# Where layer 3's transposed input comes from: TensorE transposes, or blocks read back from DRAM and turned by VectorE one pipeline stage later

## The chip, the cores and the metric

The kernel runs as one program on one core of a Trainium2 chip. The metric is the device time of one launch in microseconds; lower is better. A profiled execution adds a trace, from which the rows below come.

## What is computed

64 graphs of 256 nodes with 256 features pass through four residual layers, each followed by a layer norm. Layer 0 is a recurrence over the 256 nodes; layers 1 to 3 work on each graph by itself. Only layers 1 to 3 matter here:

```python
x = _layernorm(x + L0(x, adj, ...))                 # recurrence over nodes
x = _layernorm(x + relu(norm_adj @ (x @ W.T + b)))  # layer 1
x = _layernorm(x + L2(x, adj, ...))                 # layer 2: one head, masked softmax
# layer 3: 8 heads, masked softmax
q = split_heads(x @ Wq + bq)
k = split_heads(x @ Wk + bk)
v = split_heads(x @ Wv + bv)
scores = jnp.einsum('bhqd,bhkd->bhqk', q, k) / np.float32(np.sqrt(HD))
scores = jnp.where(adj[:, None, :, :] > 0, scores, jnp.float32(NEG))
out = jnp.einsum('bhqk,bhkd->bhqd', jax.nn.softmax(scores, axis=-1), v)
x = _layernorm(x + out.reshape(...) @ Wo + bo)
```

Layer 3's three projections need the layer's input with features on the partitions, that is, transposed: `x` arrives as 256 nodes by 256 features.

## The kernel before, in words

The program has two parts. `_recurrence` does layer 0 for all graphs and writes its result to a DRAM tile `Hd`; it ends at about 1424 us of the trace. `_layers` then does layers 1 to 3, in fp32, and is the part that changes. (A third function, `_layer_3`, is a safe version of layer 3 that reads the DRAM tile `Yd`; it runs only where a flag says so, and did not run here.)

`_layers` is a software pipeline written out by hand. One `Graph` object holds a graph's tiles, and each of its methods issues one step. A string `ROUND` lists the steps of one round in order, as `stage.step`, and a loop over `t` issues a round after another; the scheduler is switched off (`manual_schedule`), so each engine's queue runs in exactly this order. In round `t` the stage letter says which graph a step belongs to: `N` is graph t+2, `L` t+1, `A` t, `B` t-1, `C` t-2, `E` t-3. So six graphs are in flight:

- `load_a` and `load_b` (N) bring a graph's data in. `load_blocks` (lines 1095 to 1105) loads a 256x256 matrix as 8 DMAs of 32 KB, in such a way that each 32x32 block lands at the place of its mirror image; one VectorE instruction that transposes every 32x32 block then gives the whole transpose. This is how layer 1's input (`hz`, `xz`, turned in `turn_0`, line 1112) and the adjacency (`az`, turned in `adT_v`, line 1143) are transposed today.
- L: residual and norm of layer 0, degrees, adjacency; A: layer 1 (`t_a`, `t_b`, `g`); B: layer 2 (`xT.2`, `qk2`, `v2`, `s2`, `exp2`, `w2`, `pT2`, `f2`).
- C: layer 3's first half. `norm_b.2` writes layer 3's input `y`; `keep_3` (line 1252) stores it to `Yd`; `xT.3` (`flipped`, line 1038, four TensorE transposes of 128x128 into a PSUM bank, and the ScalarE copy at line 1164) transposes it; `qk3` (line 1240) and `v3` project, `s3` (lines 1274, 1283, 1284, 1286) makes scores, mask and exponentials for four heads at a time.
- E: layer 3's second half: `o3`, `d3`, `f3`, norm, `store`.

All DMAs of this part are issued from SyncE's queue (SP), in program order: in a round the store of E, `load_a`, `keep_3`, `load_b`. Each product (`product`, line 1048: eight matmul records of one 256x256x256 product) takes one of four PSUM banks (`bank`), in turn.

Of the kernel before, what the change touches and what calls it, by code (L numbers as in the profile page):

```python
# [9 lines left out]
F32 = mybir.dt.float32  # L10
# [9 lines left out]
P = 128  # L20
# [934 lines left out]
def _layers(tc, ident, Hd, Yd, x, adj, weights, out):  # L955
# [8 lines left out]
    nc = tc.nc  # L964
    nat, W2, W3, b1_r, b2_r, b3_r, cols = weights
    B, N, D = x.shape
# [5 lines left out]
    with ExitStack() as ctx:  # L972
# [9 lines left out]
        io = ctx.enter_context(tc.tile_pool(name="l_io", bufs=3))  # L982
# [71 lines left out]
        def new(tag, t, bufs=2, shape=(P, 2, D)):  # L1054
            return work.tile(list(shape), F32, tag=tag, name=f"{tag}_{t}", bufs=bufs)
# [17 lines left out]
        class Graph:  # L1073
# [7 lines left out]
            def load_a(self):  # L1081
                b = self.b
                self.xin = io.tile([P, 2, D], F32, tag="xin", name=f"xin_{b}")
                nc.sync.dma_start(self.xin, x[b].rearrange("(c p) d -> p c d", p=P))
                self.ad = io.tile([P, 2, N], F32, tag="ad", name=f"ad_{b}", bufs=4)
                nc.sync.dma_start(self.ad, adj[b].rearrange("(c p) m -> p c m", p=P))
                self.y = io.tile([P, 2, D], F32, tag="y", name=f"y_{b}", bufs=7)
                nc.sync.dma_start(self.y, Hd[:, b, :].rearrange("(c p) d -> p c d", p=P))
                self.az = self.load_blocks("az", adj[b])

# [1 line left out]
                self.hz = self.load_blocks("hz", Hd[:, self.b, :])  # L1092
                self.xz = self.load_blocks("xz", x[self.b])

            def load_blocks(self, tag, of):

                to = io.tile([P, 2, 8, 32], F32, tag=tag, name=f"{tag}_{self.b}", bufs=3)
                for j in range(4):
                    for a in range(2):
                        at = a * P + j * 32  # L1100
                        nc.sync.dma_start(
                            to[j * 32:(j + 1) * 32, a],
                            of[:, at:at + 32].rearrange("(i r) c -> r i c", r=32),
                        )
                return to


            def residual_0(self):
                nc.gpsimd.tensor_add(self.y, self.y, self.xin)
                nc.gpsimd.tensor_add(self.hz, self.hz, self.xz)  # L1110

            def turn_0(self):
                self.xT0 = new("xT0", self.b)
                nc.vector.transpose(
                    self.xT0.rearrange("p a m -> p (a m)"),
                    self.hz.rearrange("p a i c -> p (a i c)"),
                )

            def norm_a(self, l):
                self.mv = norm_a(self.y, f"{l}_{self.b}")  # L1120
# [21 lines left out]

            def adT_v(self):

                self.turned = new("adTr", self.b)
                nc.vector.transpose(
                    self.turned.rearrange("p a m -> p (a m)"),
                    self.az.rearrange("p a i c -> p (a i c)"),
                )
                self.neg3 = new("neg3", self.b, 4)  # L1150
                nc.vector.tensor_scalar(self.neg3, self.turned, 0.0, -NEG, ALU.is_le, ALU.mult)

            def adT_s(self):
# [96 lines left out]
                setattr(self, f"qk3{s}", m)  # L1250

            def keep_3(self):
                nc.sync.dma_start(Yd[self.b], self.y)

            def bias_3(self):
                nc.gpsimd.tensor_add(self.y, self.y, rows(b3_r))
# [82 lines left out]
        ROUND = """  # L1339
            B.xT.2 E.o3 E.d3.0 B.qk2.0 C.norm_b.2 E.d3.1  # L1340
            A.t_a A.t_b B.qk2.1 B.v2 L.residual_0 B.masks L.degrees_a
            L.adT_v E.f3 L.degrees_b C.xT.3 C.keep_3 N.load_b
            L.adT_s A.g C.bias_3 L.norm_a.0
            C.qk3.0 C.qk3.1 E.norm_a.3 A.norm_a.1 L.norm_b.0 B.s2 B.exp2
            C.s3.0 C.v3 B.w2
            B.pT2 A.norm_b.1 L.turn_0 C.s3.1 E.norm_b.3 E.store B.f2
            B.norm_a.2
        """.split()
        graphs = [Graph(b) for b in range(B)]
        graphs[0].load_a()  # L1350
        graphs[0].load_b()
        for t in range(-1, B + 3):
            if 0 <= t + 2 < B:
                graphs[t + 2].load_a()
            for step in ROUND:
                who, name, *args = step.split(".")
                b = t - "NLABCE".index(who) + 2
                if 0 <= b < B:
                    getattr(graphs[b], name)(*map(int, args))

# [33 lines left out]
def _layer_3(tc, ident, Yd, adj, l3, out):  # L1394

    nc = tc.nc
    B, N, D = out.shape
    HEADS = 8
    HD = D // HEADS
    with ExitStack() as ctx:  # L1400
# [32 lines left out]
        def rows(b):  # L1433
            return b.unsqueeze(1).to_broadcast([P, 2, D])

        with tc.For_i(0, B, 1) as b:
            y = work.tile([P, 2, D], F32, name="gy")
            nc.sync.dma_start(y, Yd[b])
            ad = work.tile([P, 2, N], F32, name="gad")
            nc.sync.dma_start(ad, adj[b].rearrange("(c p) m -> p c m", p=P))  # L1440
            neg = work.tile([P, 2, N], F32, name="gneg")
            nc.vector.tensor_scalar(neg, ad, 0.0, -NEG, ALU.is_le, ALU.mult)
            xT = flip(y, "gxT")
            qk = []
            for s, n in enumerate("qk"):
                pm = product(W[n], xT, f"g{n}_ps")
                m = work.tile([P, 2, N], F32, name=f"g{n}")
                for c in range(2):
                    nc.vector.tensor_scalar(m[:, c, :], pm[:, c, :], cols[:, s, c:c + 1], None, ALU.add)
                qk.append(m)  # L1450
            v = work.tile([P, 2, D], F32, name="gv")
            nc.vector.tensor_add(v, product(xT, W["v"], "gv_ps"), rows(row["v"]))
            o = work.tile([P, 2, D], F32, name="go")
            for h in range(HEADS):
                hc, i = divmod(h, P // HD)
                r = slice(i * HD, (i + 1) * HD)
                pm = ps.tile([P, 2, N], F32, tag="mm", name=f"gs_ps_{h}")
                for c in range(2):
                    nc.tensor.matmul(
                        pm[:, c, :], qk[0][r, hc, c * P:(c + 1) * P], qk[1][r, hc, :],  # L1460
                        start=True, stop=True,
                    )
                sm = work.tile([P, 2, N], F32, tag="gs", name=f"gs_{h}")
                nc.vector.tensor_add(sm, pm, neg)
                mx = work.tile([P, 2], F32, tag="gmx", name=f"gmx_{h}")
                nc.vector.tensor_reduce(mx, sm, AX.X, ALU.max)
                sums = work.tile([P, 2], F32, tag="gsums", name=f"gsums_{h}")
                for c in range(2):
                    nc.vector.tensor_scalar(
                        sm[:, c, :], sm[:, c, :], mx[:, c:c + 1], None, ALU.subtract  # L1470
                    )
                nc.scalar.activation(sm, sm, AF.Exp, scale=1.0 / math.sqrt(HD))
                nc.vector.tensor_reduce(sums, sm, AX.X, ALU.add)
                nc.vector.reciprocal(sums, sums)
                pT = flip(sm, "gpT")
                po = ps.tile([P, 2, HD], F32, tag="po", name=f"go_ps_{h}")
                for c in range(2):
                    for k in range(2):
                        nc.tensor.matmul(
                            po[:, c, :], pT[:, k, c * P:(c + 1) * P],  # L1480
                            v[:, k, h * HD:(h + 1) * HD], start=(k == 0), stop=(k == 1),
                        )
                    nc.vector.tensor_scalar(
                        o[:, c, h * HD:(h + 1) * HD], po[:, c, :], sums[:, c:c + 1], None, ALU.mult
                    )
            pm = product(flip(o, "goT"), W["o"], "gf_ps")
            nc.gpsimd.tensor_add(y, y, rows(row["o"]))
            nc.vector.tensor_add(y, y, pm)
            for c in range(2):
                st = work.tile([P, 6], F32, tag="gst", name=f"gst_{c}")  # L1490
                mv = work.tile([P, 2], F32, tag="gmv", name=f"gmv_{c}")
                rstd = work.tile([P, 1], F32, tag="grstd", name=f"grstd_{c}")
                nc.vector.bn_stats(st, y[:, c, :])
                nc.vector.bn_aggr(mv, st)
                nc.vector.tensor_scalar(rstd, mv[:, 1:2], EPS, None, ALU.add)
                nc.gpsimd.tensor_tensor(rstd, rstd, mhalf[:, 0:1], ALU.pow)
                nc.vector.tensor_scalar(
                    y[:, c, :], y[:, c, :], mv[:, 0:1], rstd, ALU.subtract, ALU.mult
                )
            nc.sync.dma_start(out[b].rearrange("(c p) d -> p c d", p=P), y)  # L1500
# [3 lines left out]
def kernel(ctx: ExitStack, tc: tile.TileContext, ins, out):  # L1504
    nc = tc.nc
    x, adj = ins["x"], ins["adj"]
    B, N, D = x.shape
    main = ctx.enter_context(tc.tile_pool(name="main", bufs=1))
    dram = ctx.enter_context(tc.tile_pool(name="dram", bufs=1, space=bass.MemoryType.DRAM))
# [18 lines left out]
        )),  # L1528
        wide, load_layers,
    )  # L1530
    Yd = dram.tile([B, P, 2, D], F32, name="Yd")
    found = _layers(tc, ident, Hd, Yd, x, adj, weights, out)
    with tc.If(found > 0):
        _layer_3(tc, ident, Yd, adj, l3, out)
# [36 lines left out]
```

## Time and profile before

| | us |
|---|---|
| median of 3 runs | 3260.26 (3257.63 to 3262.72) |
| the profiled execution, its own time | 3263.34 |
| its span, first to last instruction | 3261.6 |
| end of the recurrence's last matmuls in the trace | 1423 |
| one round of the layers, full pipeline | 27.50 |
| busy share of the span: PE, DVE, ACT, POOL | 94%, 79%, 61%, 58% |
| busy share of 2400 to 2600 us: PE, DVE, ACT, POOL | 100%, 89%, 66%, 53% |

PE is TensorE (PEld its weight loads), DVE VectorE, ACT ScalarE, POOL GpSimd, SPq SyncE's DMA queue. The spans of the whole program mix two parts with different limits, so a change in the layers is read in rows from that part: from about 1440 us on, in rounds.

### The profile page before, as it was taken

Reading aid. Unit: us, or ns where it says so; the run is one execution under the profiler, and the core shown is the slowest. Engines: PE = TensorE matmul, PEld = TensorE weight load, DVE = VectorE, ACT = ScalarE, POOL = GpSimd, SP = SyncE. Lnnn points to the kernel's source line nnn. Section 1 sums busy time; section 2 is a strip of 40 time slices with the busy share of each in tenths; the row PEclk is TensorE's granted clock in tenths of the full one; section 3 lists DMA queues with packets and bytes.
Section 4 is the critical chain, followed back from the end, with each engine's and each line's share of the span. In section 5 each row is a group of like instructions: output and inputs, shape, how many; then the busy total and the mean of one; then the engine's idle time right before and its main releaser. Section 6 shows DMA issues by size and latency. Waiting matters only on the chain.

```text
span 3261.6 us, 80661 instructions
## 1 busy us (share of the span) xinstructions
PE 3057.9 (94%) x28332; PEld 2274.2 (70%) x28332; DVE 2585.9 (79%) x7361; ACT 1987.3 (61%) x5224; POOL 1884.5 (58%) x2226
## 2 busy tenths in 40 slices
PE   4799999999899998959999999999999999999997
PEld 3566666655566655637888888888888888888885
DVE  2477777877677878746888888888988888888885
ACT  0166666666566666635666666666666666666664
POOL 2276777777677878724555555555555555555543
PEclk8899999999999999979999999999999999999999
DMA  9866777787776764333333333333333333333310
GB/s 304 245 166 147 191 175 184 168 181 195 174 190 149 189 157 134 90 73 80 75 75 76 75 78 78 79 78 79 78 79 79 79 79 78 79 77 79 77 42 21
DMA packets 806735, 385.76 MB, mean 118 GB/s; under 512 B 525260, under 2 KB 774232, under 8 KB 802648
## 3 DMA queue, kind: packets, MB, share of 16 engines
q1 hardware_dynamic: 788312, 362.61, 46.3%
q10 hardware_dynamic: 18016, 17.96, 1.7%
q8 instruction: 226, 3.70, 0.5%
q14 instruction: 181, 1.48, 0.2%
HBM read 261.75 MB, written 99.61 MB: 111 GB/s over the span
## 4 chain that ended last, share of the span: by engine, by line
PE 82%; DMA 7%; DVE 6%; issue 2%; SPq 1%; ACT 1%; POOL 1%; ACTq 0%; DVEq 0%; POOLq 0%
PE mm L1048 14%; PE rc L620 7%; PE rc L612 5%; PE s L1274 4%; PE late L531 4%; PE mm_2f L1048 4%; PE mm_3v L1048 4%; PE mm_2v L1048 3%; PE mm_3f L1048 3%; PE mm_t L1048 3%; PE mm_g L1048 3%; PE mm_2s L1048 3%; PE mm_2w L1048 3%; PE o L1309 3%; PE z_ps L620 3%; PE z_ps L612 2%
## 5 line engine op out<-in xcount | busy, mean ns | idle before, releaser
L1286 POOL TENSOR_TENSOR p3s<-p 128x256 f32<-128x256 f32 x512 | 359.1, 734 | 269.2 <-ACT p L1284 269.0
L1048 PE MATMUL mm<-xT,weights 128*128 128x256 f32 x2048 | 484.0, 385 | 2.7 <-ACT xT L1164 2.7
L696 POOL TENSOR_TENSOR ACC<-ACC,far 128x640 f32<-128x640 f32 (+2 forms) x312 | 413.4, 1325 | 83.0 <-ACT far L687 44.9
L645 DVE SCALAR_TENSOR_TENSOR ACC<-keep,S,ACC 128x128 f32<-128x128 f32 x1561 | 436.8, 343 | 14.4 <-POOL ACC L913 9.6
L1048 PEld LDWEIGHTS mm<-xT,weights 128*128 128x128 f32 x2048 | 386.2, 191 | 80.3 <-ACT xT L1164 29.3
L1283 DVE TENSOR_TENSOR p<-s,neg 128x512 f32<-128x512 f32 x512 | 317.5, 682 | 85.2 <-PE s L1274 85.2
L1004 ACT ACTIVATE y<-y,shift,rstd 128x256 f32<-128x256 f32 x512 | 279.6, 596 | 158.6 <-DVE shift L1002 158.5
L1284 ACT ACTIVATE p<-p 128x512 f32<-128x512 f32 x512 | 306.9, 629 | 3.3 <-DVE p L1283 3.0
L612 PE MATMUL rc<-WxT,xqT 128*64 128x256 f32 x2048 | 268.8, 383 | 4.3 <-ACT xqT L256 2.2
L996 POOL TENSOR_TENSOR rstd<-rstd,mhalf 128x2 f32<-128x2 f32 x256 | 173.9, 698 | 134.1 <-DVE rstd L995 132.3
L840 POOL TENSOR_TENSOR ready<-ACC,dinv 128x128 f32<-128x128 f32 x255 | 102.3, 401 | 251.9 <-DVE ACC L645 246.4
L692 POOL TENSOR_TENSOR far<-hs,S 128x384 f32<-128x384 f32 (+1 forms) x310 | 222.5, 718 | 4.7
L1323 DVE RECIPROCAL rT<-o 128x256 f32<-128x256 f32 x128 | 223.7, 1748 | 0.0
L992 DVE BATCH_NORM_STATS2 st<-y 128x6 f32<-128x256 f32 x512 | 209.6, 409 | 12.6 <-POOL y L1185 9.8
L1185 POOL TENSOR_TENSOR y<-y,g 128x512 f32<-128x512 f32 x64 | 81.2, 1269 | 216.4 <-ACT g L1182 190.2
L1196 ACT ACTIVATE qk<-mm,weights 128x256 f32<-128x256 f32 x256 | 107.4, 470 | 160.4 <-PE mm L1048 158.6
L620 PE MATMUL rc<-WhT,rT 128*64 128x128 f32 x2048 | 170.2, 287 | 29.7 <-DVE rT L863 27.7
L620 PE MATMUL rc<-WhT,xpT 128*64 128x128 f32 x2048 | 168.9, 286 | 29.3 <-ACT xpT L629 27.7
L863 DVE TENSOR_TENSOR rT<-rT_ps,xpT 128x128 f32<-128x128 f32 x256 | 74.2, 290 | 153.8 <-PE rT_ps L861 150.6
L531 PE MATMUL late<-Hw,An 64*32 64x256 f32 x3840 | 172.0, 390 | 19.4 <-DMA Hw<-hs 7.8
L620 PEld LDWEIGHTS rc<-WhT,rT 128*64 128x64 f32 x2048 | 107.9, 137 | 117.1 <-DVE rT L863 110.8
L620 PEld LDWEIGHTS rc<-WhT,xpT 128*64 128x64 f32 x2048 | 107.0, 136 | 115.1 <-ACT xpT L629 106.1
(170 smaller groups left out, 7413.1 us busy)
## 6 DMA issues: line engine op xcount, KB each, us to landing
xX<-in_x_dram ACTq DMA_DIRECT2D x16, 1024.0 KB
Us<-xu SPq DMA_DIRECT2D x64, 256.0 KB
ACC<-Us SPq DMA_DIRECT2D x32, 512.0 KB
Es<-eu SPq DMA_DIRECT2D x64, 256.0 KB
early_sb<-Es SPq DMA_DIRECT2D x32, 512.0 KB
xin<-in_x_dram SPq DMA_DIRECT2D x64, 256.0 KB
ad<-in_adj_dram SPq DMA_DIRECT2D x64, 256.0 KB
y<-Hd SPq DMA_DIRECT2D x64, 256.0 KB
```

The costliest lines, as they stand in the source:

```text
L531: nc.tensor.matmul(pb[g][q * T:(q + 1) * T, e, :], An[rows, b].rearrange("p u s -> p (u s)"), Hw[rows, b, :], start=True, stop=True,)
L612: nc.tensor.matmul(G[o * B:(o + 1) * B], xqT[a, i // 2][:, i % 2, kc, h * B:(h + 1) * B], WxT[:, kc, o, gates], start=False, stop=False, s ...
L620: nc.tensor.matmul(G[o * B:(o + 1) * B], hT[:, kc * B:(kc + 1) * B], WhT[:, kc, o, g], start=False, stop=(kc == 1), skip_group_check=True,)
L645: nc.vector.scalar_tensor_tensor(acc[:, 0, :], keep[:, j % 2, :], s, acc[:, 0, :], ALU.mult, ALU.add)
L692: nc.gpsimd.tensor_mul(tmp[:, begun:count, :], hs.unsqueeze(1).to_broadcast(shape), s[:, begun:count].unsqueeze(2).to_broadcast(shape),)
L696: nc.gpsimd.tensor_add(acc, acc, tmp[:, 0:count, :])
L1004: nc.scalar.activation(y[:, c, :], y[:, c, :], AF.Identity, bias=shift[:, c:c + 1], scale=rstd[:, c:c + 1],)
L1048: nc.tensor.matmul(pm[:, c, :], lhsT[:, k, c * P:(c + 1) * P], rhs[:, k, :], start=(k == 0), stop=(k == 1),)
L1283: nc.vector.tensor_add(p, s_ps[i], self.neg3)
L1284: nc.scalar.activation(p, p, AF.Exp, scale=ISQ)
L1286: nc.gpsimd.tensor_add(both, p[:, 0, :], p[:, 1, :])
L1323: nc.vector.reciprocal(rT, o_ps[:, 1, :])
```

## The change

Stage C no longer projects. After it has stored `y` to `Yd`, which now has the plain layout of nodes by features, `load_3` reads it back with `load_blocks` as 8 DMAs of 32 KB into a new tile `yz`, and `turn_3` turns its blocks with one VectorE instruction, right behind layer 1's `turn_0` and before the second group of scores. The four TensorE transposes and the ScalarE copy of `xT.3` are gone. A new stage `D` (graph t-3) takes over `qk3`, `s3` and `v3`, and `E` becomes graph t-4; the loop runs one round more, and `y` and `neg3` have one more buffer. The transposition of `hz` and `az` goes through a common helper `turn`, with the same instruction as before.

```diff
-                self.y = io.tile([P, 2, D], F32, tag="y", name=f"y_{b}", bufs=7)
+                self.y = io.tile([P, 2, D], F32, tag="y", name=f"y_{b}", bufs=8)
...
+            def turn(self, tag, blocks):
+                t = new(tag, self.b)
+                nc.vector.transpose(
+                    t.rearrange("p a m -> p (a m)"), blocks.rearrange("p a i c -> p (a i c)")
+                )
+                return t
...
-                self.neg3 = new("neg3", self.b, 4)
+                self.neg3 = new("neg3", self.b, 5)
...
             def keep_3(self):
-                nc.sync.dma_start(Yd[self.b], self.y)
+                nc.sync.dma_start(Yd[self.b].rearrange("(c p) d -> p c d", p=P), self.y)
+
+            def load_3(self):
+                self.yz = self.load_blocks("yz", Yd[self.b], 2)
+
+            def turn_3(self):
+                self.xT_sb = self.turn("xT3", self.yz)
...
         ROUND = """
             B.xT.2 E.o3 E.d3.0 B.qk2.0 C.norm_b.2 E.d3.1
             A.t_a A.t_b B.qk2.1 B.v2 L.residual_0 B.masks L.degrees_a
-            L.adT_v E.f3 L.degrees_b C.xT.3 C.keep_3 N.load_b
-            L.adT_s A.g C.bias_3 L.norm_a.0
-            C.qk3.0 C.qk3.1 E.norm_a.3 A.norm_a.1 L.norm_b.0 B.s2 B.exp2
-            C.s3.0 C.v3 B.w2
-            B.pT2 A.norm_b.1 L.turn_0 C.s3.1 E.norm_b.3 E.store B.f2
+            L.adT_v E.f3 L.degrees_b C.keep_3 N.load_b
+            L.adT_s A.g C.load_3 C.bias_3 L.norm_a.0
+            D.qk3.0 D.qk3.1 E.norm_a.3 A.norm_a.1 L.norm_b.0 B.s2 B.exp2
+            D.s3.0 D.v3 B.w2
+            B.pT2 A.norm_b.1 L.turn_0 C.turn_3 D.s3.1 E.norm_b.3 E.store B.f2
             B.norm_a.2
         """.split()
...
-        for t in range(-1, B + 3):
+        for t in range(-1, B + 4):
...
-                b = t - "NLABCE".index(who) + 2
+                b = t - "NLABCDE".index(who) + 2
...
-    Yd = dram.tile([B, P, 2, D], F32, name="Yd")
+    Yd = dram.tile([B, N, D], F32, name="Yd")
```

More of the change, by code (lines that the diff above doesn't have):

```diff
@@ L1093, in load_b, with load_blocks @@
                 self.xz = self.load_blocks("xz", x[self.b])
-            def load_blocks(self, tag, of):
-                to = io.tile([P, 2, 8, 32], F32, tag=tag, name=f"{tag}_{self.b}", bufs=3)
+            def load_blocks(self, tag, of, bufs=3):
+                to = io.tile([P, 2, 8, 32], F32, tag=tag, name=f"{tag}_{self.b}", bufs=bufs)
                 for j in range(4):
@@ L1110, in residual_0 @@
                 nc.gpsimd.tensor_add(self.hz, self.hz, self.xz)
-            def turn_0(self):
[L1113 to L1117, printed above, removed]
+            def turn(self, tag, blocks):
[4 more added lines that the diff above has]
+                return t
+            def turn_0(self):
+                self.xT0 = self.turn("xT0", self.hz)
             def norm_a(self, l):
@@ L1143, in adT_v @@
             def adT_v(self):
[L1145 to L1149, printed above, removed]
-                self.neg3 = new("neg3", self.b, 4)
+                self.turned = self.turn("adTr", self.az)
+                self.neg3 = new("neg3", self.b, 5)
                 nc.vector.tensor_scalar(self.neg3, self.turned, 0.0, -NEG, ALU.is_le, ALU.mult)
@@ L1437, in _layer_3 @@
             y = work.tile([P, 2, D], F32, name="gy")
-            nc.sync.dma_start(y, Yd[b])
+            nc.sync.dma_start(y, Yd[b].rearrange("(c p) d -> p c d", p=P))
             ad = work.tile([P, 2, N], F32, name="gad")
```

## The prediction

> **What bounds the kernel now.** First the page: the whole span, then the 40 slices, to find the part that changes.
>
> ```profile
> span 3261.6 us, 80661 instructions
> ...
> PE 3057.9 (94%) x28332; PEld 2274.2 (70%) x28332; DVE 2585.9 (79%) x7361; ACT 1987.3 (61%) x5224; POOL 1884.5 (58%) x2226
> ...
> PE   4799999999899998959999999999999999999997
> DMA  9866777787776764333333333333333333333310
> ```
>
> From slice 18 on (the layers) PE stands at 9 and DMA at 3. The busy time by stretch says how full the others are there:
>
> ```profile
> 2400.00:2600.00 200.00, 200.00 (x1354) 162.75 (x1353) 179.00 (x436) 131.72 (x282) 105.50 (x130) 1.00 0.34 80
> ```
>
> PE is never idle, DVE has 10% left, the granted clock is 1.00. A busy PE alone proves little, so next the timeline of one round on PE:
>
> ```profile
> 2324.60 1.89 PE L1048 MATMUL mm_g<-t,adT 128*128 128x256 f32 x8
> ...
> 2337.84 1.99 PE L1048 MATMUL mm_2f<-w,pT 128*128 128x256 f32 x8
> ...
> 2349.94 1.89 PE L1048 MATMUL mm_3f<-weights,oT 128*128 128x256 f32 x8
> 2351.66 0.60 PE L1038 MATMUL tr_x<-ident,y 128*128 128x128 f32 x4
> 2352.10 1.89 PE L1048 MATMUL mm_g<-t,adT 128*128 128x256 f32 x8
> ```
>
> mm_g to mm_g is 27.50 us, the round, and no PE row between carries a wait. PE is the bound, and the tr_x group between mm_3f and mm_g is what goes. How close the others follow is on DVE's and ACT's timelines:
>
> ```profile
> 2331.71 0.69 DVE L1217 TENSOR_TENSOR sm<-mm_2s,ad 128x512 f32<-128x512 f32 x1 [0.17 <-PE mm_2s L1048]
> ...
> 2336.01 0.70 DVE L1114 STREAM_TRANSPOSE xT<-hz 128x512 f32<-128x512 f32 x1
> 2337.93 2.48 DVE L1283 TENSOR_TENSOR p<-s,neg 128x512 f32<-128x512 f32 x4 [1.22 <-PE s L1274]
> ...
> 2352.03 0.71 DVE L1146 STREAM_TRANSPOSE adTr<-az 128x512 f32<-128x512 f32 x1 [0.21 <-DMA hz<-Hd]
> ```
> ```profile
> 2337.12 0.60 ACT L1230 COPY pT<-tr_p 128x512 f32<-128x512 f32 x1
> ```
>
> DVE's one real gap is 1.22 us before the second scores, right behind turn_0's transpose (2336.01): the place of turn_3. And ACT ends pT at 2337.72, only 0.12 before mm_2f needs it. Last the DMA queue, and the DMA engines a round later:
>
> ```profile
> 2348.41 0.37 SPq L1253 DMA_DIRECT2D Yd<-y  x1
> 2348.82 3.92 SPq L1101 DMA_DIRECT2D hz<-Hd  x8
> ```
> ```profile
> 2385.00:2386.00 1.00, 1.00 (x6) 0.89 (x5) 0.79 (x4) 0.83 (x2) 1.00 (x2) 1.00 0.42 67
> 2386.00:2387.00 1.00, 1.00 (x12) 0.63 (x14) 0.45 (x2) 0.43 (x1) 1.00 (x3) 1.00 0.04 6
> ```
>
> The second column from the right is the DMA share: it dies at 2386.0. Call T the start of the second scores on DVE (2337.93, then 2365.43). keep_3 is issued at T+10.48; two groups of eight block loads follow at 0.49 us each and end at T+18.75, which is 2384.18 in the next round. So the last block lands about 1.85 us after its issue.
>
> **The change part by part.**
>
> *PE: four transposes less per graph.* The groups list puts tr_x at 276 ns each, and the Trainium skill ("TensorE: Matmul & The Clock Gate", Part 4) names about 275 ns for one in a kernel. By that, four are 1.1 us and 60 full rounds 66 us. But a mean of one is not a share of the queue: mm_3f starts at 2349.94, a product takes 1.73 start to start, tr_x starts at 2351.66 and mm_g at 2352.10. Pipelined, the four cost 0.44 us. The row decides: 27.50 falls to 27.06 at best.
>
> *ACT: one copy of 0.59 less.* ACT stood idle 1.32 us just before it, so nothing is gained there. The bank that it used goes too: of 15 banks a round 14 stay, and mm_g then takes the bank that t_a's product left, which it must await anyway for t (done by 2350.64, needed at 2351.66).
>
> *DVE: one transpose of 0.70 more* (the row of turn_0, same shape). Today adT_v's transpose is held 0.21 for its eight DMA semaphores; in the order of the built kernel that wait has gone, and turn_3 carries it. DVE's own loop: 27.50 - 1.22 - 0.17 (both waits for PE) + 0.70 = 26.81. It still fits under 27.06, with 0.25 to spare. Behind turn_3 on DVE stand the second scores; for them wait ACT's exponentials, POOL's sums and PE's o3.
>
> *The mixed chain.* The same layers tie the engines crosswise: PE's second scores (end 2337.84) release DVE (0.09); DVE reaches s2 after 21.28 - 0.17 - 0.21 = 20.90; from s2 to the end of pT are 2337.72 - 2331.71 = 6.01; 0.12 to mm_2f; then one PE round of 27.06 to the scores after. Sum 54.18 for two rounds, 27.09 each. So of 0.44 about 0.41 remains. Ends: 0.44 (the 0.12 is slack) and 0.30 (adT_v's 0.21 stays). I take 0.40: 60 full rounds (t = 4 to 63) give 24.0.
>
> *SP and DMA: eight block loads more.* They stand behind load_b and before E's store. keep_3 must have landed: hz's eighth DMA today already waits for it on the same semaphore and loses nothing (3.92 for eight), so it lands in under 3.9 us. Its rows shrink from 2 KB to 1 KB; E's store has 1 KB rows and lands in time for the same wait. SP is then issuing until T+22.65; the next store is at T+4.21 of the round after (2342.14), so 8 us stay free. yz lands at T+22.65+1.85 = T+24.5. turn_3 is reached at about T+25.9 (s2 at 20.9, plus 2336.71 - 2331.71 = 5.0). Margin 1.4 us. The Trainium skill ("DMA: Bandwidth & Descriptors", Rules for kernel authors) speaks against this: small transfers are to be coalesced, since under 64 KB one pays mostly overhead, and the page's fixed cost of a DMA is about 2.0 us (fitted on GpSimd's path). Paid in series, an estimate from that page, eight cost 16 us, yz lands at T+34.8 and each round loses 9 us: slower by over 500 us. The row says that eight go out in 3.9 us and overlap, and the DMA share is 0.42 beside such loads. I take the row. It has a spread, though: in the round 1555 one group of eight took 5.26, and more than a quarter of the groups took over 4.0. Three groups lie between keep_3 and turn_3, so some rounds use up the margin. I charge 3 us for these in all (ends 0 and 10).
>
> *A stage more: fill and drain.* Rounds are counted from xT.2 to xT.2 (o3 in the drain):
>
> ```profile
> 1490.21 1.06 PE L1038 MATMUL tr_x<-ident,y 128*128 128x128 f32 x4
> ...
> 1514.46 0.60 PE L1038 MATMUL tr_x<-ident,y 128*128 128x128 f32 x4
> ```
> ```profile
> 3217.73 0.64 PE L1300 MATMUL o<-p3s,ones 128*32 128x256 f32 x8
> ...
> 3243.10 0.76 PE L1300 MATMUL o<-p3s,ones 128*32 128x256 f32 x8 [0.53 <-DVE p L1283]
> ```
>
> Round 2 takes 24.25 today. It loses layer 3's projections and scores (8 us of PE), but its softmax of layer 2 is then exposed, as in round 1 (25.52, with cold products of 3.78): estimate 23.0, so -1.3. Round 3 becomes today's round 2 without the transposes: 23.8 for 27.50, so -3.7. Round 64 loses the exposed transposes and copy, 3204.14 - 3202.87: -1.2. Round 65 took 25.37; without xT.3 (3229.48 to 3231.21) and with PE no longer cold after it (16 qk3 records took 5.89, warm 3.62): about 22.3, so -3.1. The new round has D and E of the last two graphs: o3 to mm_3f's second half as at the end of today (3243.10 to 3249.97, 6.9), its rest 1.6, qk3 3.6, then copies, scores and sums to the next o3, about 6: +18. Sum +8.7; ends +5 and +14.
>
> **Sum.** -24.0 + 8.7 + 3 = -12.3. Against the span 3261.6 that gives 3249.3 (own time 3263.34, 1.7 more). That execution lies 3.1 above the median; taken from the median, 3260.3 - 12.3 = 3248.0.
>
> **The rivals.** (1) *yz comes late.* turn_3 waits in DVE's queue, the second scores behind it, and PE stalls at o3. It decides where a block lands more than 1.85 + 1.4 + 0.25 = 3.5 us after its issue; every further microsecond costs 60. For it: the y load of 256 KB took 4.6 us in the fill, and the margin is small. Against: the DMA share falls to 0.04 at once after the blocks, and the queue would be alone then. At 4.6 us, 1.1 late: the round is 28.2, 60 x 0.7 + 8.7 = +51, 3311. At break-even (0.2 us late) 3260.
>
> (2) *The gain is eaten by the mixed chain.* DVE has 0.25 to spare, and some of its small instructions stretch beside POOL's (shift 0.16 to 0.76). If 0.3 of the 0.44 is lost to such shifts, 60 x 0.14 = 8.4 pays for the fill and drain only: 3260 to 3262. With all lost, 3269.
>
> (3) *PE takes all 0.44 and SP's spread is hidden:* -26.4 + 8.7 = -17.7, 3242.6.
>
> That the transposes stay is excluded: the built kernel's PE order has 64 groups of them fewer.
>
> **How the numbers follow.** About 0.2% (6.5 us) is what a measurement of this kernel can tell from no change. The forecast, with rival 3 at its lower end, has 0.64: 3240 to 3254. Rival 2 in the middle 0.13 (same); rival 2 entirely lost 0.09 and rival 1 0.14 (slower). Faster 0.64, same 0.13, slower 0.23. The range goes from 3240 (rival 3 with the fill and drain at their low end, less a little) to 3267 (near rival 2 lost); about 0.05 lies below, 0.15 above.
>
> **What would show it.** Right: mm_g starts 1.73 after mm_3f; the round is 27.05 to 27.2; turn_3 takes 0.70 and its wait is 0.2 to 0.3; adT_v's wait is gone; the last round is about 18 us longer in the drain. Wrong: a wait of turn_3 for yz of over half a microsecond in most rounds (rival 1); PE rows with waits for pT, for o3's sums or for xT.2's copy (rival 2); a new round of over 22 us in the drain.

## The result, and the profile after

The changed kernel takes 3242.68 us (median of 7 runs, 3236.6 to 3248.55); the kernel before, run again beside it, takes 3259.58 (3253.68 to 3268.86). The ratio is 0.9942 [0.9925, 0.9958]: faster by 0.58%, some 19 us by the ratio and 17 by the two medians. The forecast was 3248.0, a gain of 12.3. The profiled execution of the changed kernel has a span of 3239.9 us and an own time of 3241.76.

The page after (span; busy time, share of the span and instruction count by engine; the slices of PE and DMA):

```profile
span 3239.9 us, 80388 instructions
...
PE 3038.5 (94%) x28076; PEld 2257.2 (70%) x28076; DVE 2611.5 (81%) x7425; ACT 1949.4 (60%) x5160; POOL 1882.3 (58%) x2226
...
PE   4799999999999998958999999999999999999997
DMA  9866777777776764434344444444444444444421
```

PE has 256 matmul records less, four for each of 64 graphs, DVE 64 instructions more and ACT 64 less. The DMA slices of the layers rose from 3 to 4. The stretch from 2400 to 2600 us (busy time of PE, PEld, DVE, ACT and POOL, then the granted clock, the DMA share and GB/s):

```profile
2400.00:2600.00 200.00, 200.00 (x1374) 162.32 (x1366) 184.75 (x448) 129.45 (x278) 107.31 (x133) 1.00 0.41 92
```

PE is still never idle and its granted clock is still 1.00. DVE's busy time rose from 179.00 to 184.75. PE's timeline of one round after (start, busy time, operation):

```profile
2328.19 1.89 PE L1048 MATMUL mm_3f<-weights,oT 128*128 128x256 f32 x8
2329.92 1.89 PE L1048 MATMUL mm_g<-t,adT 128*128 128x256 f32 x8
...
2343.16 1.99 PE L1048 MATMUL mm_2f<-w,pT 128*128 128x256 f32 x8
...
2355.26 1.89 PE L1048 MATMUL mm_3f<-weights,oT 128*128 128x256 f32 x8
...
2356.98 1.89 PE L1048 MATMUL mm_g<-t,adT 128*128 128x256 f32 x8
```

mm_g starts 1.73 after mm_3f, where it was 2.16 with the transposes between them, and mm_g to mm_g is 27.06. DVE's timeline of that round, of the next, and up to s2 in the one after:

```profile
2329.93 0.70 DVE L1114 STREAM_TRANSPOSE adTr<-az 128x512 f32<-128x512 f32 x1
...
2337.03 0.69 DVE L1216 TENSOR_TENSOR sm<-mm_2s,ad 128x512 f32<-128x512 f32 x1
...
2341.27 0.70 DVE L1114 STREAM_TRANSPOSE xT<-hz 128x512 f32<-128x512 f32 x1
2341.90 0.66 DVE L1114 STREAM_TRANSPOSE xT<-yz 128x512 f32<-128x512 f32 x1
2343.25 2.48 DVE L1288 TENSOR_TENSOR p<-s,neg 128x512 f32<-128x512 f32 x4 [0.68 <-PE s L1279]
...
2364.09 0.69 DVE L1216 TENSOR_TENSOR sm<-mm_2s,ad 128x512 f32<-128x512 f32 x1
...
2369.80 0.71 DVE L1114 STREAM_TRANSPOSE xT<-yz 128x512 f32<-128x512 f32 x1 [0.77 <-DMA yz<-Yd]
2370.44 2.45 DVE L1288 TENSOR_TENSOR p<-s,neg 128x512 f32<-128x512 f32 x4
...
2391.16 0.69 DVE L1216 TENSOR_TENSOR sm<-mm_2s,ad 128x512 f32<-128x512 f32 x1
```

adT_v's wait of 0.21 is gone. turn_3 sits in the gap ahead of the second scores, and 0.68 us of that gap is still there. The third group of rows shows the next round, in which the block loads come late: turn_3 waits 0.77, and the scores follow at once, without a wait of their own. The lateness used up the gap and 0.13 us more (2343.25 to 2370.44 is 27.19), and DVE made that up before s2: 20.72 us from the scores to s2, where it had taken 20.84 a round earlier (2343.25 to 2364.09). PE's next round is 27.07. Over the steady part, 1600 to 3100 us, the list of waits has (us in total, times, longest):

```profile
DVE p L1288 <- PE s L1279: 30.1, 47, 0.7
...
DVE xT L1114 <- DMA yz<-Yd: 4.8, 8, 0.9
```

DVE waits for PE 47 times and for the read-back 8 times; three more waits of turn_3, 1.2 us together, stand in the list without a named releaser. PE leads.

**Where the 19 us lie in the two traces.** From the first xT.2 to the end the layers took 1796.9 us before and 1777.9 after: 19.0 less. The 60 full rounds have a mean of 27.506 before and 27.075 after, which makes 25.8; fill and drain give 6.8 back. The recurrence, which the change does not touch, ended 1.9 us earlier in this trace. Its last matmuls ended between 1411.4 and 1429.8 us in the traces of the kernels that share it, so single runs differ by several microseconds for that alone.

The fill and the drain (PE rows of the changed kernel; xT.2 of rounds 2, 3 and 4, then o3 of the last three rounds):

```profile
1487.31 1.06 PE L1038 MATMUL tr_x<-ident,y 128*128 128x128 f32 x4
...
1509.09 0.60 PE L1038 MATMUL tr_x<-ident,y 128*128 128x128 f32 x4
...
1532.45 0.60 PE L1038 MATMUL tr_x<-ident,y 128*128 128x128 f32 x4
```
```profile
3180.93 0.64 PE L1305 MATMUL o<-p3s,ones 128*32 128x256 f32 x8
...
3203.41 0.70 PE L1305 MATMUL o<-p3s,ones 128*32 128x256 f32 x8 [0.53 <-DVE p L1288]
...
3221.24 0.69 PE L1305 MATMUL o<-p3s,ones 128*32 128x256 f32 x8 [0.53 <-DVE p L1288]
```

Round 2 takes 21.78 (24.25 before), round 3 23.36 (27.50), round 65 22.48 (25.37), and the new round 17.83.

### The profile page after: what moved, and what is told of

It reads as the page before. It is cut to its first block, busy times and chain, and to the rows that moved or that the text cites. A ratio compares the mean times of both kernels' runs of the same rounds, so it can differ in the third digit from the quotient of the medians.

```text
span 3239.9 us, 80388 instructions
## 1 busy us (share of the span) xinstructions
PE 3038.5 (94%) x28076; PEld 2257.2 (70%) x28076; DVE 2611.5 (81%) x7425; ACT 1949.4 (60%) x5160; POOL 1882.3 (58%) x2226
## 4 chain that ended last, share of the span: by engine, by line
PE 83%; DVE 6%; DMA 5%; issue 2%; SPq 1%; POOL 1%; ACT 1%; ACTq 0%; DVEq 0%; POOLq 0%
PE mm L1048 14%; PE rc L620 8%; PE rc L612 5%; PE late L531 4%; PE s L1279 4%; PE mm_2f L1048 4%; PE mm_3v L1048 4%; PE mm_2v L1048 3%; PE mm_t L1048 3%; PE mm_g L1048 3%; PE mm_3f L1048 3%; PE mm_2s L1048 3%; PE mm_2w L1048 3%; PE o L1314 3%; PE z_ps L620 3%; PE z_ps L612 3%
```

## The experiments

All ratios are to the kernel before, run on the same chip, with a 95% interval.

**1. The stage alone.** Stage D and the extra round stay, but the TensorE transposes come back and nothing is read back or turned.

```diff
-            L.adT_v E.f3 L.degrees_b C.keep_3 N.load_b
-            L.adT_s A.g C.load_3 C.bias_3 L.norm_a.0
+            L.adT_v E.f3 L.degrees_b C.xT.3 C.keep_3 N.load_b
+            L.adT_s A.g C.bias_3 L.norm_a.0
...
-            B.pT2 A.norm_b.1 L.turn_0 C.turn_3 D.s3.1 E.norm_b.3 E.store B.f2
+            B.pT2 A.norm_b.1 L.turn_0 D.s3.1 E.norm_b.3 E.store B.f2
```

> Stage D and the extra round stay, but the four TensorE transposes and the ScalarE copy of layer 3's input are kept in stage C, and nothing is read back. My theory: the gain comes from the 0.44 us that the transposes take in PE's queue, the extra stage only costs. Then the full round is back at 27.50 us, and the layers are longer than before by the fill and drain alone: rounds 2 and 3 shorter by 2 to 6 us together, rounds 64 and 65 by 2 to 4, the new round 17 to 18 longer. In all +7 to +10 us against the kernel before, ratio 1.002 to 1.003. Rival: the gain comes from the stage itself, since the projections no longer wait for a transpose made just ahead of them; then the round falls below 27.3 here too and the kernel is faster than before.

Measured: 1.0040 [1.0022, 1.0058], 3274.13. PE's timeline:

```profile
2319.90 1.89 PE L1048 MATMUL mm_g<-t,adT 128*128 128x256 f32 x8
...
2345.24 1.89 PE L1048 MATMUL mm_3f<-weights,oT 128*128 128x256 f32 x8
...
2347.40 1.89 PE L1048 MATMUL mm_g<-t,adT 128*128 128x256 f32 x8
```

The round is 27.50 again and mm_3f to mm_g 2.16. So the stage by itself is a pure cost, some 12 us by its trace and 12 by its median, rather more than the sum's 8.7; all of the gain comes from the transposes that leave PE's queue. (The ScalarE copy came back with them. But the whole difference, 2.16 against 1.73, lies between the starts of mm_3f and mm_g, where mm_3f and the transposes alone stand.)

**2. The read-back left out.** turn_3 turns the blocks of `y` itself, so it waits for no DMA. Layer 3's input is then not the true transpose; its shape and cost are the same.

```diff
-            L.adT_s A.g C.load_3 C.bias_3 L.norm_a.0
+            L.adT_s A.g C.bias_3 L.norm_a.0
...
-                self.xT_sb = self.turn("xT3", self.yz)
+                self.xT_sb = new("xT3", self.b)
+                nc.vector.transpose(
+                    self.xT_sb.rearrange("p a m -> p (a m)"),
+                    self.y.rearrange("p a m -> p (a m)"),
+                )
```

> As the changed kernel, but nothing is read back: turn_3 turns the blocks of y as they stand in SBUF (so layer 3's input is not properly transposed: its values are left out of account, its shape and cost are the same). It takes away the eight block loads per graph and their wait. My theory: the read-back is hidden, so the round stays 27.06 to 27.07 and the time is that of the changed kernel within 2 us (ratio to before 0.994). The prediction charged 3 us for late blocks; if that charge is real, this kernel is 3 to 10 us faster than the changed one (ratio 0.991 to 0.993).

Measured: 0.9950 [0.9931, 0.9969], 3245.91; mean round 27.10. Taking away 512 DMAs gains nothing that these intervals, some 6 us to each side, can show. But one thing came with it: adT_v's wait for its DMA semaphores, gone in the changed kernel, is back, at 0.20 us in most rounds. So the price of the read-back alone is better read in the trace of the changed kernel: of its 60 full rounds three are over 27.1: 27.50 (round 4), 27.15 and 27.13, each behind a turn_3 that came late, by 1.27, 0.85 and 0.84 us. That is 0.6 us in all, where 3 us had been charged. (Round 4 takes 27.06 here, without the read-back.)

Some rounds of this run are longer still. DVE's row of one of them, then PE's:

```profile
2333.56 0.71 DVE L1114 STREAM_TRANSPOSE adTr<-az 128x512 f32<-128x512 f32 x1 [0.56 <-DMA hz<-Hd]
```
```profile
2346.53 1.99 PE L1048 MATMUL mm_2f<-w,pT 128*128 128x256 f32 x8 [0.28 <-ACT pT L1229]
```

This is the mixed chain of the forecast, seen at its edge: DVE is held ahead of s2, pT is late, and PE waits for it. In most rounds, with the wait of 0.20, DVE needs 20.95 us from the second scores to s2, mm_2f starts 0.05 behind pT's end, and the chain gives (0.09 + 20.95 + 6.01 + 0.05 + 27.06) / 2 = 27.08; the median round is 27.09.

**3. Turned twice.** One more block transpose in DVE's gap.

```diff
+                self.turn("xT3b", self.yz)
                 self.xT_sb = self.turn("xT3", self.yz)
```

> As the changed kernel, but turn_3 turns its blocks twice into two tiles, so VectorE has 0.63 to 0.70 us more in the same gap. It asks how far VectorE is from being the bound. In the changed kernel's trace VectorE still waits 0.68 us for the second scores. My theory: VectorE's own loop is 27.06 - 0.68 = 26.4 and becomes 27.0 to 27.1 with the second turn, so the round grows by at most 0.05 us, in all 0 to 3 us over the changed kernel. The prediction's sum had 26.81 for this loop, which would give 27.5 and +26 us over the changed kernel.

Measured: 0.9956 [0.9939, 0.9974], 3245.73. The mean round is 27.15, and most rounds are 27.06 or 27.07; the 60 full rounds take 4.4 us longer than in the changed kernel, a little over the 0 to 3 expected. DVE's timeline:

```profile
2339.97 0.66 DVE L1114 STREAM_TRANSPOSE xT3b<-yz 128x512 f32<-128x512 f32 x1
2340.57 0.66 DVE L1114 STREAM_TRANSPOSE xT<-yz 128x512 f32<-128x512 f32 x1
2341.32 2.48 DVE L1289 TENSOR_TENSOR p<-s,neg 128x512 f32<-128x512 f32 x4
```

The gap before the scores is now full, yet most rounds stay where PE puts them. VectorE was not the bound in the changed kernel: it had about one more transpose to spare, as the 0.68 said. What is lost lies in the rounds with a late read-back, for which no cover is left. The latest one of the steady part:

```profile
2720.76 0.71 DVE L1114 STREAM_TRANSPOSE xT3b<-yz 128x512 f32<-128x512 f32 x1 [1.16 <-DMA yz<-Yd]
```

The round that PE begins behind it, at 2722.62, takes 28.05. (In the fill one turn is 1.70 late, and round 4 behind it takes 28.54.)

**4. The same work, placed early in the next round.** turn_3 stands ahead of adT_v, with a third buffer for `yz`; the instructions are the same ones.

```diff
-            L.adT_v E.f3 L.degrees_b C.keep_3 N.load_b
+            D.turn_3 L.adT_v E.f3 L.degrees_b C.keep_3 N.load_b
...
-            B.pT2 A.norm_b.1 L.turn_0 C.turn_3 D.s3.1 E.norm_b.3 E.store B.f2
+            B.pT2 A.norm_b.1 L.turn_0 D.s3.1 E.norm_b.3 E.store B.f2
```

> As the changed kernel, but turn_3 is moved: it is done in the next round ahead of adT_v's transpose (yz has three buffers), so the same instruction stands in VectorE's queue before s2 instead of behind it. VectorE's total is unchanged and yz is there long before. My theory, the mixed chain: from the second scores to s2 VectorE then needs 20.84 + 0.70 + about 0.2 for the wait = 21.7, and (0.09 + 21.7 + 6.01 + 0.12 + 27.06) / 2 = 27.5 per round: the whole gain of the transposes is lost, +26 us over the changed kernel, ratio to before 1.002; PE rows show a wait for pT ahead of mm_2f in every other round. Rival: only each engine's own loop counts, PE 27.06 and VectorE under 27; then the round stays 27.06 and the time is that of the changed kernel.

Measured: 1.0002 [0.9989, 1.0014], 3264.10: the whole gain is gone, although PE and DVE do the same work. PE's timeline over three rounds:

```profile
2302.15 1.99 PE L1048 MATMUL mm_2f<-w,pT 128*128 128x256 f32 x8 [0.93 <-ACT pT L1229]
...
2329.21 1.99 PE L1048 MATMUL mm_2f<-w,pT 128*128 128x256 f32 x8
...
2356.91 1.99 PE L1048 MATMUL mm_2f<-w,pT 128*128 128x256 f32 x8 [0.57 <-ACT pT L1229]
```

27.06, then 27.70, in turn: every second round PE waits for pT. DVE's timeline ahead of the last row, and ScalarE's row of pT, show where it comes from:

```profile
2329.30 2.48 DVE L1288 TENSOR_TENSOR p<-s,neg 128x512 f32<-128x512 f32 x4 [1.28 <-PE s L1279]
...
2343.34 0.71 DVE L1114 STREAM_TRANSPOSE xT<-yz 128x512 f32<-128x512 f32 x1 [0.20 <-DMA hz<-Hd]
...
2350.85 0.69 DVE L1216 TENSOR_TENSOR sm<-mm_2s,ad 128x512 f32<-128x512 f32 x1
```
```profile
2356.26 0.60 ACT L1229 COPY pT<-tr_p 128x512 f32<-128x512 f32 x1
```

From the second scores to s2 DVE now needs 21.55 us (2329.30 to 2350.85), where 20.72 were enough in the changed kernel: turn_3 and its wait lie inside the chain instead of in the gap behind it. pT ends at 2356.86, and PE, which waits for it, starts mm_2f 0.05 later. The chain gives (0.09 + 21.55 + 6.01 + 0.05 + 27.06) / 2 = 27.38, the mean round measured. The theory's 27.5 had taken 21.7 and 0.12 for two of these. That the chain binds is shown by PE's wait for pT in every second round; the sum says how much it takes.

**5 and 6. The read-back made late.** Four, then eight, more block loads are issued ahead of those of `yz`, into a tile that nothing reads.

```diff
             def load_3(self):
+                more = io.tile([P, 2, 8, 32], F32, tag="yw", name=f"yw_{self.b}", bufs=2)
+                for j in range(2):
+                    for a in range(2):
+                        at = a * P + j * 32
+                        nc.sync.dma_start(
+                            more[j * 32:(j + 1) * 32, a],
+                            Yd[self.b][:, at:at + 32].rearrange("(i r) c -> r i c", r=32),
+                        )
                 self.yz = self.load_blocks("yz", Yd[self.b], 2)
```

(`range(4)` in the second.)

> As the changed kernel, but load_3 issues four more block loads of the same graph (32 KB each, into a tile that nothing reads) ahead of yz's eight. It makes yz later by 4 x 0.49 = 1.96 us and changes nothing else. My theory: in the changed kernel yz lands at about T+25.4 and turn_3 is reached at T+25.7, so yz is now 1.6 us late; VectorE has 0.68 us to spare before the second scores, and the rest goes on the round: 27.06 + 0.9 = 28.0, in 60 rounds about +55 us over the changed kernel, ratio to before 1.010 to 1.014, with turn_3 waiting 1.5 us in nearly every round. Rival: the block loads drain faster than they are issued and the lateness is smaller than the issue time; then under +25 us.

> The same with eight more block loads ahead of yz, 3.92 us. My theory: each microsecond of lateness past the spare costs 60 us, so another 1.96 us on the round against four more: 29.9 to 30.0, about +170 us over the changed kernel, ratio to before 1.045 to 1.050. Rival: the loop through SyncE's queue closes (the store of E waits, load_a and keep_3 come later, and yz with them), and the cost grows faster than the added issue time: over +200 us.

Measured: 1.0164 [1.0144, 1.0185], 3314.97, with four; 1.0522 [1.0504, 1.0541], 3432.63, with eight. SP's timeline with four more, and the turn behind it on DVE's:

```profile
2333.79 1.93 SPq L1259 DMA_DIRECT2D yw<-Yd  x4
2335.77 5.06 SPq L1101 DMA_DIRECT2D yz<-Yd  x8
```
```profile
2342.47 0.71 DVE L1114 STREAM_TRANSPOSE xT<-yz 128x512 f32<-128x512 f32 x1 [1.79 <-DMA yz<-Yd]
```

The last load was issued at 2340.83 and the turn ran at 2342.47, 1.64 later. The waits, first with four more loads, then with eight:

```profile
DVE xT L1114 <- DMA yz<-Yd: 98.6, 51, 3.1
```
```profile
DVE xT L1114 <- DMA yz<-Yd: 190.8, 49, 5.1
```

That is 1.93 and 3.89 us a round. Less DVE's gap of 0.68, times 60: 75 and 193 us over the changed kernel. Measured, by the ratios: 0.0222 and 0.0580 of 3260, 72 and 189. From four to eight the ratio rises by 0.0358, 117 us, for 1.96 us more of issue: 60 for each, the price that rival 1 was given. Both ratios came out above what was expected of them, since turn_3 waits longer than was thought: 1.93 us with four more, where 1.5 was expected. Rival 1's mechanism exists and its price was right; the change stops just short of the point from which it decides.

**7. A further version: layer 2's input in the same way.** xT.2's transposes leave PE too (another stage X, another eight loads, another turn, two more rounds in all than before; the block tiles have two buffers instead of three, and load_b comes last). DVE is relieved: the degrees' row sums go to ScalarE and neg3 to GpSimd.

```diff
+            def load_2(self):
+                self.yz2 = self.load_blocks("yz2", Yd[self.b], 2)
+
+            def turn_2(self):
+                self.xT_sb = self.turn("xT2", self.yz2)
...
-                nc.vector.tensor_reduce(deg, self.ad, AX.X, ALU.add)
+                junk = work.tile([P, N], F32, tag="junk", name=f"junk_{b}", bufs=1)
+                for c in range(2):
+                    nc.scalar.activation(junk, self.ad[:, c, :], AF.Copy, accum_out=deg[:, c:c + 1])
...
-            B.xT.2 E.o3 E.d3.0 B.qk2.0 C.norm_b.2 E.d3.1
+            E.o3 L.sums E.d3.0 B.qk2.0 C.norm_b.2 E.d3.1
...
-            B.pT2 A.norm_b.1 L.turn_0 C.turn_3 D.s3.1 E.norm_b.3 E.store B.f2
+            B.pT2 A.norm_b.1 A.keep_2 L.turn_0 X.turn_2 C.turn_3 D.s3.1 E.norm_b.3 E.store B.f2
```

> A version that carries the change on: layer 2's input is stored, read back and turned by VectorE in the same way (one more stage X, load_2 behind keep_3, load_b last), so xT.2's four transposes leave PE too. VectorE is relieved in return: the degrees' row sums go to ScalarE, neg3 to GpSimd. My theory: PE's round is 27.06 - 0.53 = 26.53; from the second scores to s2 VectorE needs about 20.84 - 0.71 - 0.34 = 19.8, so the mixed chain gives (0.09 + 19.8 + 6.01 + 0.12 + 26.53) / 2 = 26.3, below PE's round; VectorE's own loop is 26.4 - 1.05 + 0.65 = 26.0. 60 rounds x 0.53 = -32 us, the further stage +9 to +13: about -20 us against the changed kernel, ratio to before 0.987 to 0.990. Rival: SyncE's queue, busy 22.6 of 26.5 us a round then, or late blocks become the bound; then the round stays above 27 us and the kernel is slower than the changed one by the stage alone, about +10 us.

Measured: 0.9937 [0.9919, 0.9955], 3245.63: no better than the changed kernel, and neither the theory nor its rival expected it. The theory took 0.53 for xT.2's transposes, from their start to o3's. But mm_2f to o3 is 1.93 without them and was 2.36 with them (2343.16 to 2345.52 in the changed kernel), so 0.43 to 0.44 is what leaves the queue; and the round is 26.91, not 27.06 - 0.44 = 26.62. PE's timeline, and GpSimd's:

```profile
2333.08 0.64 PE L1319 MATMUL o<-p3s,ones 128*32 128x256 f32 x8
...
2335.26 0.89 PE L1319 MATMUL o<-p3s,ones 128*32 128x256 f32 x8
2336.08 1.13 PE L1048 MATMUL mm<-xT,weights 128*128 128x256 f32 x4
```
```profile
2332.67 2.81 POOL L1305 TENSOR_TENSOR p3s<-p 128x256 f32<-128x256 f32 x4 [1.96 <-ACT p L1303]
```

GpSimd's sums end at 2335.48, after PE reaches the second group of o3 at 2335.26; that group takes 0.89 where it took 0.61 in the changed kernel. In the changed kernel xT.2's transposes stood ahead of o3 and gave GpSimd their 0.44 us. So the instructions that left look like cover for another chain, which the next run puts to the test.

**8. The same with cover put back.** Layer 2's first projection goes ahead of o3.

```diff
-            E.o3 L.sums E.d3.0 B.qk2.0 C.norm_b.2 E.d3.1
+            B.qk2.0 E.o3 L.sums E.d3.0 C.norm_b.2 E.d3.1
```

> As the version with both inputs read back, but B.qk2.0 is issued ahead of E.o3. In that version's trace the round is 26.91 us, not 26.53: the transposes of xT.2 had covered the chain from the second scores over VectorE, ScalarE and GpSimd to o3's last sums, and without them o3's sums take 0.90 instead of 0.61 us and wait for GpSimd. A product of 1.73 us that depends on none of these now stands in that place. My theory: the wait goes and the round falls to 26.5 to 26.6, 60 x 0.35 = about -20 us against that version: ratio to before 0.987 to 0.989, about 0.6% below the changed kernel. Rival: o3 comes 1.73 us later, d3 and with it mm_3f come late, and the round stays at 26.9 or grows.

Measured: 0.9882 [0.9864, 0.9900], 3225.61: faster than both kernels. PE's timeline:

```profile
2323.24 1.99 PE L1048 MATMUL mm_2f<-w,pT 128*128 128x256 f32 x8
2325.07 1.89 PE L1048 MATMUL mm<-xT,weights 128*128 128x256 f32 x8
2326.89 0.64 PE L1319 MATMUL o<-p3s,ones 128*32 128x256 f32 x8
...
2329.07 0.61 PE L1319 MATMUL o<-p3s,ones 128*32 128x256 f32 x8
...
2349.86 1.99 PE L1048 MATMUL mm_2f<-w,pT 128*128 128x256 f32 x8
```

o3's second group is back at 0.61 and the round is 26.62, 0.44 under the changed kernel: again the queue time of four transposes. The 0.29 that run 7 lacked came back with the cover alone. Runs 7 and 8 carry several edits at once; what the moves to ScalarE and GpSimd are worth singly was not tried.

## Why the prediction was right, and where its sizes were off

The direction and the main mechanism were right: the gain is four transposes' share of PE's queue, paid for by a longer fill and drain. The time came out near the low end of the range.

- *Four transposes are 0.44 us of PE's queue, not 1.1.* Right. The 60 full rounds gave 25.8 us, 0.43 each; run 1 puts the transposes back and the 0.43 with them, and run 8 takes four others out for 0.44. At their mean duration of 276 ns the gain would have been 66 us.
- *The mixed chain leaves 0.40.* The chain exists, and runs 2 and 4 make it bind. In the changed kernel it does not bind: the usual round takes all of the 0.44, so a term of 24.0 measured 26.4 (25.8 with the late rounds, which belong to a term below). With the distances read there its sum is (0.09 + 20.84 + 6.01 + 0.12 + 27.06) / 2 = 27.06, but that proves nothing: the first four run from one mm_2f to the next, and add up to a round whatever bounds it. Two of them hold slack. From the scores to s2 20.72 is enough when DVE is late, and mm_2f can start 0.05 behind pT (run 4). Without the slack the chain is 26.97, 0.09 under PE's own 27.06. The forecast took 20.90 for the one and the full 0.12 for the other; that the 0.12 is slack was its upper end, and that is nearer the truth. (It also took 27.10 where its own working said 27.09.)
- *DVE's own loop of 26.81.* Too high by at least 0.4: the scores still wait 0.68 in a round of 27.06, so the loop is under 26.4. Part of it is that turn_3 starts 0.63 after turn_0, where the row had 0.70, and that adT_v's wait, left in the sum, is gone. turn_3 did not take that wait over: in the usual round it shows none of the 0.2 to 0.3 that were named as a sign. Run 3 confirms the spare time.
- *yz lands at T+24.5, margin 1.4.* Wrong, without consequence. The issue of `yz` ends at T+23.9 in the median round (T+22.7 to T+25.0; T is the start of the second scores on DVE), where T+22.65 was expected: the working took two groups that ended at T+18.75, close to the earliest of that trace, where the median is T+19.7. With four more loads, where the turn follows the landing in every round, the turn starts a median of 1.6 us after the last issue (1.85 was forecast), though 2.9 and 3.3 in two of 53. So yz is there at about T+25.5, and turn_3 is reached at T+25.7: a margin of 0.2. Groups of eight stretch, too: 20 of 64 groups of yz took over 4.0 us. So turn_3 waits in 11 rounds of the steady part, at most 0.9, and DVE's gap takes nearly all of that. That the read-back costs next to nothing is in part luck: two errors, the loop too long and the margin too wide, cancelled.
- *3 us for SP's spread and late blocks.* Too much: 0.6 in the trace, as told at run 2.
- *The transfers overlap and do not pay a fixed cost in series.* Right. Eight go out in 3.9 us and the last is there 1.6 us later; the serial estimate of 9 us a round does not hold here.
- *Fill and drain +8.7.* Measured +6.8 in the trace. Rounds 2 and 3 gave 6.6 where 5.0 was estimated (which of their waits went was not tested); round 64 gave 1.45 for 1.2, round 65 2.9 for 3.1 (the forecast's two parts, 1.73 and 2.27, really add up to 4.0), and the new round cost 17.83 for 18. Run 1 gives about 12 for the same stage with the transposes in, so the term depends on what else the edge rounds hold.

The three terms of the sum, chain, edges and spread, erred by 2.4, 1.9 and 2.4 us to the same side, together 6.7, the difference between the sum (-12.3) and the layers' traces (-19.0). Rival 3 (3242.6, all of the 0.44 taken and the spread hidden) is what happened, but for the 0.6 and the shorter edges. Rival 1 was near: four more loads make it the result.

## What to carry to other kernels

The mean duration of an instruction in a full queue (276 ns for a transpose here) is not what its removal gains (0.11 us each); what it gains is read from the starts of its neighbours, how far apart they are with it and without it. Where two engines tie each other over two rounds, add the chain up from rows before moving anything, and take out of each distance the wait or slack that it holds, for the distances of a full pipeline always add up to its round. Here the same 0.70 us instruction cost nothing in the gap behind the chain and the whole gain inside it. And before an instruction is taken off the bounding engine, ask which other engine it was giving time to.

## What the hardware showed that was not expected

- Of two block transposes in a row on VectorE the second starts 0.60 to 0.63 after the first and is listed with 0.66, where one alone takes 0.70.
- neg3 (a comparison with zero and a multiplication, 128x512) takes 1.93 us on GpSimd in run 7, while another tensor_scalar of the same shape (an addition and a multiplication) takes 0.62 there:

```profile
2340.49 0.62 POOL L1194 TENSOR_SCALAR neg<-ad 128x512 f32<-128x512 f32 x1
2344.99 1.93 POOL L1155 TENSOR_SCALAR neg<-adTr 128x512 f32<-128x512 f32 x1
```

- The issue of eight DMAs takes 3.90 us in most rounds and 4.0 to 5.5 in the others, and a few loads land over a microsecond later than usual: the turn that waits for them starts 3.1 us after the last issue in one of the 11 late rounds, where 1.4 to 1.9 is usual, with the DMA engines nearly idle (share 0.05 from 2368 to 2369 us, while turn_3 waited until 2369.80). What causes either was not settled.
